# Two graph layers in float32 on one core: head map and messages by seven half-size products, edges turned by DMA, a new order of the first phases

## The chip, the cores and the metric

The kernel runs on one core of a Trainium2 chip. The metric is the device time of one execution in microseconds (us). Five engines work side by side, each through its own queue in order: TensorE (PE, with its weight loads as PEld), VectorE (DVE), ScalarE (ACT), GpSimd (POOL), and SyncE (SP), which only issues DMAs here.

## The reference, cut to what matters

There are 64 graphs of 256 nodes with 512 features, and two attention layers after each other. `adj` is a symmetric boolean matrix per graph, with a true diagonal.

```python
def layer0(embs, score_mask, ...):            # 8 heads of 64
    keep = (~sm[..., 0:1]).astype(embs.dtype)
    m = embs @ map_w.T + map_b
    n = sem / norm                            # m by heads, each row to length 1
    cos_adj = ((n @ n.T) * ~sm > 0.1)
    q, k = m @ q_w.T + q_b, m @ k_w.T + k_b   # by heads
    scores = jnp.where(sm, NEG, q @ k.T / sqrt(64))
    p_attn = softmax(scores) * keep
    adj = cos_adj * p_attn
    sem_h = embs @ gcn_map_w.T + gcn_map_b
    return relu(((adj @ sem_h) @ gcn_W.T) / (adj.sum(-1) + 1))

def layer1(x, adjacency_mask, ...):           # 4 heads of 64
    sim = where(adjacency_mask, q @ k.T / 8, neg)
    return (softmax(sim) @ v) @ Wo + bo

h = relu(layernorm(x));  x = x + layer0(h, adj, ...)
h = relu(layernorm(x));  x = x + layer1(h, adj, ...)
```

Layer 0 attends where there is no edge, layer 1 where there is one.

## The kernel before, in words

Everything is float32. The order of the work is written out by hand: the Python order of the calls is the order in each engine's queue. A software pipeline runs over the graphs. `period(i)` works on up to four of them at once: graph `i` (`g`, the attention of its layer 0 and the projections of its layer 1), graph `i-1` (`b`, the attention of its layer 1 and its output), graph `i+1` (`nx`, map, messages, queries and keys of its layer 0) and graph `i+2` (`n2`, its mask, its layer norm, its transposes). There are 65 periods, of which number 1 to 62 have all of `g`, `b` and `nx`. A prologue, `first(0)` to `first(1)`, fills the pipeline.

The names that matter, in the order of one period, with the lines of the profile:

- `masks` (L286) turns the edges of `n2` by four bf16 transposes on PE into the PSUM tile `p_a`; ACT makes two bf16 masks of it, `mask1` (edges) and `mask0` (1 - edges).
- `turned` (L195, L196): transposes `p_t` of the normalized input, then ACT's relu writes `hT`.
- `spread` (L330, L334): `p_b`, then DVE writes `nT`. `products` (L351): a pair of 64-row products `sc` or `co` per 128 features, two heads side by side, each into a PSUM tile of its own. `exps` (L358, L359): ACT's exponential out of PSUM into `e`, then DVE multiplies by the mask. `halves` (L370): POOL adds the two halves of `e` into `d`. `far` (L365): DVE applies the threshold of the cosine to `e`. `far_off` (L385): POOL adds that to `d`.
- `mapped` (L205, L299, L301): 16 products of 256 columns into `p_m`, DVE adds the bias into `mT`, ACT squares.
- `left_factors` (L219 to L222): POOL makes the four sums `ss` of quarters of `mT` that `seven_products` needs.
- `messages` (L310, L311): per 128 nodes 4 products of 512 columns into `p_s`, then DVE adds the bias into `sem`.
- `queries`, `keys`: `seven_products` (L235, L244, L248, L266), a generator. A 512x512 matrix times `mT` is done as seven products of half-size blocks, each 4 products of 128x128 by 128 columns. Its steps: two products into the PSUM tile `24`, which ACT drains with a bias (`u2`, `u4`); one into tile `z`, which DVE adds to `u2`, then two into tile `53`, drained by ACT (`u5`); one into `z` again, which DVE drains into `uu`; the last into `z`. Each new product into `z` waits until DVE has read the one before.
- `values1`, `sums1`, `values`, `sums` (L377, L402, L443): the weighted sums `av`, and the softmax sums `zb` and `sm`, on PE. `norms` (L317) is `p_n`. `sums_back` (L411): four transposes `rt`. `heads_back` (L424), `result` (L457).
- `p_v`, `p_q`, `p_k` (L552, L205): the projections of layer 1. They end the period.

All PSUM tiles come from one pool, `ring`: eight banks, handed out in turn in the order of the calls. A tile therefore waits until whatever was allocated eight tiles earlier has been read.

Of the kernel before, what the change touches and what calls it, by code (L numbers as in the profile page):

```python
# [28 lines left out]
class Weights:  # L29


    def __init__(self, nc, const, a):
# [4 lines left out]
        self.wm, self.bm = self.load_w("map_wT", "wm"), self.load_b("map_b", "bm")  # L37
# [22 lines left out]
        self.wc = const.tile([P, D // P, D], F32, name="wc")  # L60
# [8 lines left out]
    def load_seven(self, key, name):  # L69


        ap = self.a[key]
        half = ap.shape[0] // 2
        t = self.const.tile([128, 7, half // 128, half], F32, name=name)
        for n, (i, j) in enumerate(((0, 0), (1, 0), (1, 1), (0, 1))):
            block = ap[i * half:(i + 1) * half, j * half:(j + 1) * half]
            self.nc.gpsimd.dma_start(out=t[:, n], in_=block.rearrange("(c p) f -> p c f", p=128))
        return t
# [31 lines left out]
    def fold(self, gws, gbb, bank):  # L110

        nc, P = self.nc, 128
        NKC = self.wc.shape[1]
        nc.vector.tensor_copy(gbb, self.gb[:, :, None].to_broadcast([P, NKC, P]))
        p = bank("p_bc", [P, NKC * P])
        for k in range(NKC):
            nc.tensor.matmul(p[:, k * P:(k + 1) * P], gbb[:, k, :], self.gt, start=True, stop=True)
        nc.vector.tensor_copy(self.bc, p)
        for c in range(NKC):
            p = bank(f"p_wc{c}", [P, NKC * P])  # L120
            for k in range(NKC):
                nc.tensor.matmul(p[:, k * P:(k + 1) * P], gws[k // 2][:, k % 2, c * P:(c + 1) * P], self.gt,
                                 start=True, stop=True)
            nc.vector.tensor_copy(self.wc[:, c, :], p)
# [3 lines left out]
def fast_path(ctx, tc, a, w, chk, out):  # L128
# [61 lines left out]
    def turned(g, tag):  # L190
        hT = sb2.tile([P, NKC, S], F32, tag="hT", name=f"hT{tag}")
# [23 lines left out]
    def left_factors(src, name):  # L215

        a = [src[:, HC * k:HC * (k + 1), t * P:(t + 1) * P] for t in range(2) for k in range(2)]
        ss = sb1.tile([P, 4, HC, P], F32, tag="ss", name=f"ss{name}")
# [6 lines left out]
    def seven_products(left, wt, bias, dst, name):  # L225
# [4 lines left out]
        def product(p, region, block, src):  # L230


            for f in range(HC):
                for c in range(HC):
# [3 lines left out]

        def biased(region, features, what):

            t = sb2.tile([P, HC, P], F32, tag=f"u{what}", name=f"u{what}{name}")
# [5 lines left out]
        def out(tokens, features, x, y):  # L247
            nc.vector.tensor_add(dst[:, HC * features:HC * (features + 1), tokens * P:(tokens + 1) * P], x, y)  # L248

        p24 = bank(f"{name}_24", [P, 2, HC, P])  # L250
# [5 lines left out]
        pz = bank(f"{name}_z", [P, HC, P])  # L256
        product("z", pz, 0, a11)
        out(0, 0, pz, p2)
        p53 = bank(f"{name}_53", [P, 2, HC, P])
# [5 lines left out]
        u4 = sb2.tile([P, HC, P], F32, tag="uu", name=f"uu{name}")  # L265
# [5 lines left out]
        out(1, 0, pz, p4)  # L271


    def edges(g):

        g.adb = sb1.tile([P, NT, S], BF16, tag="adb", name=f"adb{g.i}")
        nc.gpsimd.tensor_copy(g.adb, g.ad)
        g.keep = small.tile([P, NT], F32, tag="keep", name=f"keep{g.i}")
        nc.gpsimd.tensor_scalar(g.keep, g.ad[:, :, 0], -1.0, 1.0, op0=ALU.mult, op1=ALU.add)

    def masks(g):

        pa = bank(f"p_a{g.i}", [P, NT, S], BF16)
        for j in range(NT):
            for t in range(NT):
                nc.tensor.transpose(pa[:, j, t * P:(t + 1) * P], g.adb[:, t, j * P:(j + 1) * P], w.ident_b)  # L286
        g.mask0 = sb2.tile([P, NT * S], BF16, tag="mask0", name=f"mask0_{g.i}")
        g.mask1 = sb2.tile([P, NT * S], BF16, tag="mask1", name=f"mask1_{g.i}", bufs=3)
        paf = pa.rearrange("p j q -> p (j q)")
        nc.scalar.copy(g.mask1, paf)  # L290
        nc.scalar.activation(g.mask0, paf, AF.Copy, scale=-1.0, bias=1.0)

    def mapped(g):
        g.mT = sb1.tile([P, NKC, S], F32, tag="mT", name=f"mT{g.i}")
        g.sq = []
        for n in range(NKC // 2):
            p = features_first(w.wm, g.hT, (2 * n, 2 * n + 1), f"p_m{g.i}_{n}")
            for m in (2 * n, 2 * n + 1):
                nc.vector.tensor_scalar_add(g.mT[:, m, :], p[:, m - 2 * n, :], w.bm[:, m:m + 1])  # L299
            sq = sb2.tile([P, 2, S], F32, tag="sq", name=f"sq{g.i}_{n}")  # L300
            nc.scalar.activation(sq, g.mT[:, 2 * n:2 * n + 2, :], AF.Square)  # L301
            g.sq.append(sq)
        g.left = left_factors(g.mT, f"q{g.i}")

    def messages(g, t):
        if t == 0:
            g.sem = sb2.tile([P, NT, D], F32, tag="sem", name=f"sem{g.i}")
        p = bank(f"p_s{g.i}_{t}", [P, D])
        for c in range(NKC):
            nc.tensor.matmul(p, g.hT[:, c, t * P:(t + 1) * P], w.wc[:, c, :], start=(c == 0), stop=(c == NKC - 1))  # L310
        nc.vector.tensor_add(g.sem[:, t, :], p, w.bc)  # L311

    def norms(g):

        p = bank(f"p_n{g.i}", [P, S])
        for c in range(NKC):
            nc.tensor.matmul(p[32 * c:32 * (c + 1), :], w.blk32, g.sq[c // 2][:, c % 2, :], start=True, stop=True)  # L317
# [18 lines left out]
    def queries(g):  # L336
        g.qT = sb1.tile([P, NKC, S], F32, tag="qT", name=f"qT{g.i}")
        return seven_products(g.left, w.wq, w.bq, g.qT, f"p_q{g.i}")

    def keys(g):  # L340
        g.kT = sb1.tile([P, NKC, S], F32, tag="kT", name=f"kT{g.i}")
        return seven_products(g.left, w.wk, w.bk, g.kT, f"p_k{g.i}")
# [11 lines left out]
    def exps(ps, mask, name):  # L354
# [4 lines left out]
        nc.vector.tensor_mul(e, e, mask[:, None, :].to_broadcast([P, 2, NT * S]))  # L359
        return e  # L360

# [31 lines left out]
    def sums(g):  # L393
        sm = bank(f"sm{g.i}")
        for n in range(2):
            for k in range(4):
# [4 lines left out]
                for m, part in enumerate(parts):  # L401
                    nc.tensor.matmul(sm[32 * k:32 * (k + 1), n, :], w.ones[:, :32], part,  # L402
                                     start=(m == 0), stop=(m == len(parts) - 1))
        nc.scalar.activation(g.sms, sm, AF.Copy, accum_out=chk[:, g.i, 0:1])

    def sums_back(g):

        rt = bank(f"rt{g.i}", [P, NT, 2, P])
        for t in range(NT):
            for n in range(2):  # L410
                nc.tensor.transpose(rt[:, t, n, :], g.sms[:, n, t * P:(t + 1) * P], w.ident)  # L411
        r = small.tile([P, NT * H0], F32, tag="r", name=f"r{g.i}")
        nc.vector.reciprocal(r, rt.rearrange("p t n (k r) -> p (t n k) r", r=32)[:, :, 0])
        rc = small.tile([P, NT * H0], F32, tag="rc", name=f"rc{g.i}")
        nc.scalar.activation(rc, r, AF.Copy, accum_out=chk[:, g.i, 1:2])
        g.rk = small.tile([P, NT, H0], F32, tag="rk", name=f"rk{g.i}")
        for t in range(NT):
            nc.vector.tensor_scalar_mul(g.rk[:, t, :], r[:, t * H0:(t + 1) * H0], g.keep[:, t:t + 1])

    def heads_back(g):  # L420
        for t in range(NT):
# [3 lines left out]
            o = sb2.tile([P, H0, DH], F32, tag="o", name=f"o{g.i}_{t}")  # L425
# [22 lines left out]
    def divided(b):  # L448
        rz = b.rz = sb1.tile([P, NIC, S], F32, tag="rz", name=f"rz{b.i}")
        nc.vector.reciprocal(rz, b.z)  # L450
        b.oT = sb1.tile([P, NIC, S], F32, tag="oT", name=f"oT{b.i}")
        nc.vector.tensor_mul(b.oT, b.avs1, rz)  # L452

    def result(b, t):
        p = bank(f"p_o{b.i}_{t}", [P, D])
        for c in range(NIC):
            nc.tensor.matmul(p, b.oT[:, c, t * P:(t + 1) * P], w.wo1[:, c, :], start=(c == 0), stop=(c == NIC - 1))  # L457
        nc.vector.tensor_add(b.xs[:, t, :], p, b.xs[:, t, :])

    def period(i):  # L460
        g = graphs.get(i) if i < B else None
        b, nx, n2 = graphs.get(i - 1), graphs.get(i + 1), graphs.get(i + 2)

        if g:
            spread(g)
            for c in range(NKC):
                g.e[c] = exps(products(g.kT, g.qT, c, f"sc0_{i}_{c}"), g.mask0, f"0_{i}_{c}")
                g.d[c] = halves(g.e[c], f"0_{i}_{c}")
        if nx:
            mapped(nx)  # L470

        co, sc = {}, {}
        for c in range(NKC):
            if g:
                co[c] = products(g.nT, g.nT, c, f"co{i}_{c}")
            if b and c == 1:
                sc = [products(b.k1T, b.q1T, k, f"sc1_{b.i}_{k}") for k in range(NIC)]
            if g and c < 2:
                far_off(g, c, co[c])
        if b:  # L480
            b.e1 = [exps(sc[k], b.mask1, f"1_{b.i}_{k}") for k in range(NIC)]
# [5 lines left out]
        if nx:  # L487
            messages(nx, 0)
            q = queries(nx)
            for _ in range(3):  # L490
                next(q)
            messages(nx, 1)
            next(q, None)
# [8 lines left out]
        if g:  # L502
            g.avs = sb1.tile([P, NKC, S], F32, tag="wide", name=f"avs{i}")
            g.sms = sb1.tile([P, 2, S], F32, tag="sms", name=f"sms{i}")
# [7 lines left out]
        if b:  # L512
            nc.scalar.activation(b.z, b.rz, AF.Copy, accum_out=chk[:, b.i, 3:4])
# [16 lines left out]
        if nx:  # L530
            nc.scalar.activation(nx.rn, nx.rn, AF.Sqrt)
        if b:
# [9 lines left out]
        if nx:  # L542
            next(k, None)
# [15 lines left out]
        if n2:  # L559
            masks(n2)  # L560
            n2.hT = turned(n2, f"0_{n2.i}")

    with tc.manual_schedule():
        graphs = {0: load(0)}
# [5 lines left out]
        def first(n):  # L570
# [4 lines left out]
            masks(graphs[n])  # L575
            graphs[n].hT = turned(graphs[n], f"0_{n}")

        first(0)
        g = graphs[0]
        mapped(g)  # L580
        w.fold(gws, sb2.tile([P, NKC, P], F32, tag="o", name="gbb"), bank)
        for t in (w.wq, w.wk):
            w.finish_seven(t)
# [4 lines left out]
        messages(g, 0)  # L588
        messages(g, 1)
        q, k = queries(g), keys(g)  # L590
        for step in (q, k) * 4:
            next(step, None)
# [7 lines left out]
def general_path(ctx, tc, a, w, out):  # L600
# [13 lines left out]
    nc.sync.dma_start(out=wq, in_=a["q_wT"].rearrange("(c p) f -> p c f", p=P))  # L614
    wk = one.tile([P, NKC, D], F32, tag="gwk", name="gwk")
# [90 lines left out]

    with tc.For_i(0, B) as b:
# [15 lines left out]
        for m in range(NKC):  # L723
            p = features_first(w.wm, hT, m, f"gp_m{m}")
# [3 lines left out]
        for t in range(NT):  # L728
            p = tokens_first(w.wc, hT, t, f"gp_s{t}")
# [155 lines left out]
```

## Time and profile before

| what | value |
|---|---|
| median of 3 runs | 4013.19 us (4012.94 to 4013.34) |
| the profiled execution, its own time | 4012.99 us |
| its span, first to last instruction | 4011.2 us |
| mean granted TensorE clock | 0.997 |
| PE busy, matmuls | 3960.5 us, 26705 records |
| DVE, POOL, ACT busy | 2403.3, 1976.9, 1464.8 us |
| one period, from one `p_a` to the next | 61.48 us (2026.75 to 2088.23) |

How to read it: busy time of PE is the union of its matmul records, whose ends are modelled, so the difference of two neighbouring starts is the better measure of what a group takes on PE. A float32 matmul leaves two records, so a row "x16" of 128-column products is 8 matmuls.

### The profile page before, as it was taken

Reading aid. Unit: us, or ns where it says so; the run is one execution under the profiler, and the core shown is the slowest. Engines: PE = TensorE matmul, PEld = TensorE weight load, DVE = VectorE, ACT = ScalarE, POOL = GpSimd, SP = SyncE. Lnnn points to the kernel's source line nnn. Section 1 sums busy time; section 2 is a strip of 40 time slices with the busy share of each in tenths; the row PEclk is TensorE's granted clock in tenths of the full one; section 3 lists DMA queues with packets and bytes.
Section 4 is the critical chain, followed back from the end, with each engine's and each line's share of the span. In section 5 each row is a group of like instructions: output and inputs, shape, how many; then the busy total and the mean of one; then the engine's idle time right before and its main releaser. Section 6 shows DMA issues by size and latency. Waiting matters only on the chain.

```text
span 4011.2 us, 64377 instructions
## 1 busy us (share of the span) xinstructions
PE 3960.5 (99%) x26705; PEld 3114.0 (78%) x26705; DVE 2403.3 (60%) x3805; ACT 1464.8 (37%) x3266; POOL 1976.9 (49%) x1548
## 2 busy tenths in 40 slices
PE   7999999999999999999999999999999999999997
PEld 5877778777778777777787777877777877777775
DVE  4665565566566655665666556556656665566564
ACT  2433333333333333333343343333333333333332
POOL 3455455454454553554545545545445455354452
PEclk9999999999999999999999999999999999999998
DMA  2000000000000000000000000000000000000000
GB/s 90 12 23 12 23 12 23 23 12 23 23 12 23 17 18 23 12 23 23 12 23 23 12 23 12 23 23 12 23 23 12 23 17 18 23 12 23 23 6 17
DMA packets 56647, 82.06 MB, mean 20 GB/s; under 512 B 21984, under 2 KB 21984, under 8 KB 56352
## 3 DMA queue, kind: packets, MB, share of 16 engines
q1 hardware_dynamic: 52224, 71.32, 5.6%
q0 software_dynamic: 1856, 6.55, 0.5%
q8 instruction: 211, 3.46, 0.4%
q14 instruction: 84, 0.69, 0.1%
q10 hardware_dynamic: 2272, 0.04, 0.0%
HBM read 44.34 MB, written 33.55 MB: 19 GB/s over the span
## 4 chain that ended last, share of the span: by engine, by line
PE 96%; DVE 0%; ACT 0%; issue 0%; POOL 0%; DVEq 0%; ACTq 0%
PE p_m L205 11%; PE p_s L310 11%; PE av L377 8%; PE sc L351 8%; PE p_k L235 6%; PE co L351 6%; PE p_v L552 6%; PE p_q L235 6%; PE p_k L205 6%; PE p_q L205 6%; PE p_o L457 5%; PE p_k_z L235 4%; PE p_q_z L235 4%; PE p_t L195 3%; PE p_b L330 2%; PE sm L402 2%
## 5 line engine op out<-in xcount | busy, mean ns | idle before, releaser
L370 POOL TENSOR_TENSOR d<-e 128x512 f32<-128x512 f32 x382 | 659.4, 1751 | 1132.0 <-DVE e L359 1132.0
L359 DVE TENSOR_TENSOR e<-e,mask 128x1024 f32<-128x1024 f32 x384 | 618.4, 1665 | 164.6 <-ACT e L358 164.6
L385 POOL TENSOR_TENSOR d<-d,e 128x512 f32<-128x512 f32 x504 | 695.9, 1391 | 19.7
L428 POOL TENSOR_TENSOR xs<-xs,o 128x512 f32<-128x512 f32 x128 | 159.9, 1271 | 640.7 <-DVE o L426 640.7
L310 PE MATMUL p_s<-wc,hT 128*128 128x512 f32 x1024 | 467.0, 599 | 0.0
L205 PE MATMUL p_m<-hT,wm 128*128 128x256 f32 x2048 | 461.8, 384 | 0.7 <-ACT hT L196 0.7
L205 PEld LDWEIGHTS p_m<-hT,wm 128*128 128x128 f32 x2048 | 385.7, 191 | 72.3 <-ACT e L358 20.5
L334 DVE TENSOR_TENSOR nT<-mT,p_b 128x512 f32<-128x512 f32 x128 | 82.3, 684 | 588.1 <-PE p_b L330 588.1
L358 ACT ACTIVATE e<-sc 128x512 f32<-128x512 f32 x768 | 389.7, 617 | 68.2 <-PE sc L351 67.5
L310 PEld LDWEIGHTS p_s<-wc,hT 128*128 128x128 f32 x1024 | 184.5, 190 | 205.4 <-issue 184.7
L365 DVE SCALAR_TENSOR_TENSOR e<-co,e 128x512 f32<-128x512 f32 x512 | 317.2, 680 | 1.9 <-PE co L351 0.5
L541 POOL TENSOR_TENSOR xs<-xs,bo_b 128x512 f32<-128x512 f32 x128 | 171.2, 1356 | 174.9 <-DVE xn L186 172.1
L450 DVE RECIPROCAL rz<-z 128x512 f32<-128x512 f32 x64 | 214.6, 3353 | 71.0 <-ACT z L446 71.0
L351 PE MATMUL co<-nT 64*128 64x256 f32 x2048 | 251.5, 385 | 3.3 <-DVE e L365 3.3
L457 PE MATMUL p_o<-wo,oT 128*128 128x512 f32 x512 | 232.6, 597 | 5.0 <-DVE oT L452 5.0
L377 PE MATMUL av<-e,sem 128*64 128x256 f32 x2048 | 231.9, 379 | 0.0
L552 PE MATMUL p_v<-wv,hT 128*128 128x256 f32 x1024 | 231.7, 379 | 0.2 <-ACT hT L196 0.2
L351 PE MATMUL sc<-qT,kT 64*128 64x256 f32 x2048 | 231.7, 376 | 0.0
L205 PE MATMUL p_q<-hT,wq 128*128 128x256 f32 x1024 | 231.5, 379 | 0.0
L205 PE MATMUL p_k<-hT,wk 128*128 128x256 f32 x1024 | 231.5, 379 | 0.0
L351 PEld LDWEIGHTS co<-nT 64*128 64x128 f32 x2048 | 195.1, 188 | 44.5 <-issue 20.6
L351 PEld LDWEIGHTS sc<-qT,kT 64*128 64x128 f32 x2048 | 198.3, 187 | 22.8
(147 smaller groups left out, 6615.2 us busy)
## 6 DMA issues: line engine op xcount, KB each, us to landing
xs<-in_x_dram SPq DMA_DIRECT2D x64, 512.0 KB, 3.9
out_dram<-xs SPq DMA_DIRECT2D x64, 512.0 KB, 2.8
ad<-in_adj_dram SPq DMA_DIRECT2D x64, 64.0 KB, 3.6
wm<-in_L_gnn_map_w_dram POOLq DMA_DIRECT2D x1, 1024.0 KB, 9.3
gw<-in_L_gnn_gcn_map_w_dram POOLq DMA_DIRECT2D x2, 512.0 KB, 10.2
wq<-in_L_gnn_q_w_dram POOLq DMA_DIRECT2D x4, 256.0 KB, 12.0
wk<-in_L_gnn_k_w_dram POOLq DMA_DIRECT2D x4, 256.0 KB, 8.8
wv<-in_L_gnn_Wv_dram POOLq DMA_DIRECT2D x1, 512.0 KB, 8.5
```

Of the source, the lines that this page charges most:

```text
L205: nc.tensor.matmul(p[:, n, :], wt[:, c, m * P:(m + 1) * P], src[:, c, :], start=(c == 0), stop=(c == nk - 1))
L235: nc.tensor.matmul(region[:, f, :], wt[:, block, c, f * P:(f + 1) * P], src[:, c, :], start=p not in opened, stop=True, skip_group_check=True)
L310: nc.tensor.matmul(p, g.hT[:, c, t * P:(t + 1) * P], w.wc[:, c, :], start=(c == 0), stop=(c == NKC - 1))
L351: nc.tensor.matmul(ps[s][:, j, :], rows[h, c, j * P:(j + 1) * P], cols[h, c, :], start=True, stop=True)
L358: nc.scalar.activation(e[:, s, :], p.rearrange("p j q -> p (j q)"), AF.Exp, scale=SCALE)
L359: nc.vector.tensor_mul(e, e, mask[:, None, :].to_broadcast([P, 2, NT * S]))
L365: nc.vector.scalar_tensor_tensor(e[:, s, :], p.rearrange("p j q -> p (j q)"), THRESHOLD, e[:, s, :], op0=ALU.is_gt, op1=ALU.mult)
L370: nc.gpsimd.tensor_add(d, e[:, :, :S], e[:, :, S:])
L377: nc.tensor.matmul(av[s * DH:(s + 1) * DH, n, :], vs[:, j, (h0 + s) * DH:(h0 + s + 1) * DH], q[:, s, j * S:(j + 1) * S], start=(j == 0), s ...
L385: nc.gpsimd.tensor_add(g.d[c], g.d[c], g.e[c][:, :, j * S:(j + 1) * S])
L457: nc.tensor.matmul(p, b.oT[:, c, t * P:(t + 1) * P], w.wo1[:, c, :], start=(c == 0), stop=(c == NIC - 1))
L552: nc.tensor.matmul(p[:, t, :], hT[:, c, t * P:(t + 1) * P], w.wv1[:, c, :], start=(c == 0), stop=(c == NKC - 1))
```

## The change

- `wm` and the folded message weights `wc` are stored as seven half-size blocks like `wq` and `wk`; `mapped` and `messages` go through `seven_products`. For messages, which have the nodes first, a block product is 2 matmuls of 256 columns, and the biases are added by DVE. POOL makes the sums of quarters for `hT` too (tile `sh`; those for `mT` are now in `sm`, a tile which has nothing to do with the PSUM tile `sm` of the head sums).
- The edges of `n2`: POOL writes `adb` = 1 - edges, and SP's queue turns it by two DMA transposes into one mask. Layer 0 multiplies by it; layer 1 uses mask < 0.5 in a `scalar_tensor_tensor`. `masks` goes.
- The head sums are collected in one row of 256 per 32 partitions in place of two; `sums_back` has two transposes in place of four.
- A one-element exponential right behind the square roots; the reciprocals of layer 1 are made in place.
- Order of a period: the first step of the map ahead of `spread`, the other steps between the mask multiplications; the first step of the messages ahead of `co`; the first step of the queries ahead of `co` 2 and 3; the other steps of queries and messages in turn.
- `hT` has one buffer in place of two. The prologue folds and combines the weights in another order.

```diff
     def seven_products(left, wt, bias, dst, name, tokens_first=False):
...
         def product(p, region, block, src):
-            for f in range(HC):
-                for c in range(HC):
+            for c in range(HC):
+                if tokens_first:
+                    nc.tensor.matmul(region, src[:, c, :], wt[:, block, c, :],
+                                     start=p not in opened, stop=True, skip_group_check=True)
+                    opened.add(p)
+                    continue
+                for f in range(HC):
                     nc.tensor.matmul(region[:, f, :], wt[:, block, c, f * P:(f + 1) * P], src[:, c, :],
                                      start=p not in opened, stop=True, skip_group_check=True)
...
         def biased(region, features, what):
+            t = sb2.tile(shape, F32, tag=f"u{what}", name=f"u{what}{name}")
+            if tokens_first:
+                nc.vector.tensor_add(t, region, bias[:, features * HC * P:(features + 1) * HC * P])
+                return t
...
     def edges(g):
-        g.adb = sb1.tile([P, NT, S], BF16, tag="adb", name=f"adb{g.i}")
-        nc.gpsimd.tensor_copy(g.adb, g.ad)
+        adb = sb1.tile([P, NT, S], BF16, tag="adb", name=f"adb{g.i}")
+        nc.gpsimd.tensor_scalar(adb, g.ad, -1.0, 1.0, op0=ALU.mult, op1=ALU.add)
...
+        g.mask = sb2.tile([P, NT, S], BF16, tag="mask", name=f"mask{g.i}", bufs=3)
+        for t in range(NT):
+            nc.sync.dma_start_transpose(out=g.mask[:, :, t * P:(t + 1) * P], in_=adb[:, t, :])
...
     def mapped(g):
         g.mT = sb1.tile([P, NKC, S], F32, tag="mT", name=f"mT{g.i}")
...
+        return seven_products(g.left_h, w.wm, w.bm, g.mT, f"p_m{g.i}")
+
+    def squares(g):
...
+        g.left_m = left_factors(g.mT, "sm", g.i)
...
-    def messages(g, t):
...
+    def messages(g):
+        g.sem = sb2.tile([P, NT, D], F32, tag="sem", name=f"sem{g.i}")
+        return seven_products(g.left_h, w.wc, w.bc, g.sem, f"p_s{g.i}", tokens_first=True)
...
+    def masked(e, mask, edges):
+        m = mask.rearrange("p j q -> p (j q)")[:, None, :].to_broadcast([P, 2, NT * S])
+        if edges:
+            nc.vector.scalar_tensor_tensor(e, m, 0.5, e, op0=ALU.is_lt, op1=ALU.mult)
+        else:
+            nc.vector.tensor_mul(e, e, m)
...
     def period(i):
...
+        def off_edges(cs):
+            for c in cs if g else ():
+                masked(g.e[c], g.mask, edges=False)
+                g.d[c] = halves(g.e[c], f"0_{i}_{c}")
+        if nx:
+            m, s = mapped(nx), messages(nx)
+            next(m)
         if g:
             spread(g)
             for c in range(NKC):
-                g.e[c] = exps(products(g.kT, g.qT, c, f"sc0_{i}_{c}"), g.mask0, f"0_{i}_{c}")
-                g.d[c] = halves(g.e[c], f"0_{i}_{c}")
+                g.e[c] = exps(products(g.kT, g.qT, c, f"sc0_{i}_{c}"), f"0_{i}_{c}")
+        off_edges((0, 1))
         if nx:
-            mapped(nx)
+            next(m)
+        off_edges((2,))
+        if nx:
+            next(m)
+        off_edges((3,))
+        if nx:
+            next(s)
+            next(m)
+            squares(nx)
 
         co, sc = {}, {}
         for c in range(NKC):
             if g:
                 co[c] = products(g.nT, g.nT, c, f"co{i}_{c}")
             if b and c == 1:
                 sc = [products(b.k1T, b.q1T, k, f"sc1_{b.i}_{k}") for k in range(NIC)]
+            if nx and c == 1:
+                q = queries(nx)
+                next(q)
             if g and c < 2:
                 far_off(g, c, co[c])
         if b:
-            b.e1 = [exps(sc[k], b.mask1, f"1_{b.i}_{k}") for k in range(NIC)]
+            b.e1 = [exps(sc[k], f"1_{b.i}_{k}") for k in range(NIC)]
+            for k in range(NIC):
+                masked(b.e1[k], b.mask, edges=True)
             if not b.last:
                 b.d1 = [halves(b.e1[k], f"1_{b.i}_{k}") for k in range(NIC)]
         if g:
             far_off(g, 2, co[2])
             far_off(g, 3, co[3])
         if nx:
-            messages(nx, 0)
-            q = queries(nx)
-            for _ in range(3):
-                next(q)
-            messages(nx, 1)
-            next(q, None)
+            for step in (q, s, q, s, q, s):
+                next(step)
...
         if nx:
             nc.scalar.activation(nx.rn, nx.rn, AF.Sqrt)
+
+        nc.scalar.activation(spare[:, 1:], spare[:, :1], AF.Exp)
...
         if n2:
-            masks(n2)
-            n2.hT = turned(n2, f"0_{n2.i}")
+            normal_input(n2)
+
+    def normal_input(g):
+        g.hT = turned(g, f"0_{g.i}")
+        g.left_h = left_factors(g.hT, "sh", g.i)
```

## The prediction

> **What bounds the kernel now.** I read the busy shares and the chain of waits first.
>
> ```profile
> PE 3960.5 (99%) x26705; PEld 3114.0 (78%) x26705; DVE 2403.3 (60%) x3805; ACT 1464.8 (37%) x3266; POOL 1976.9 (49%) x1548
> ...
> PE 96%; DVE 0%; ACT 0%; issue 0%; POOL 0%; DVEq 0%; ACTq 0%
> ```
>
> PE is never without work, so PE time removed is time gained, as long as no wait takes its place. Shares over the span don't tell that; the windows of one period, cut at the start of `av` of layer 1, do (columns: length, then busy us of PE, PEld, DVE, ACT, POOL):
>
> ```profile
> 2026.75:2058.27 31.52, 31.52 (x206) 24.74 (x204) 19.97 (x25) 12.96 (x26) 24.14 (x18) 1.00 0.01 1
> 2058.27:2088.23 29.96, 29.96 (x213) 23.66 (x213) 17.38 (x34) 9.87 (x25) 6.80 (x7) 1.00 0.12 39
> ```
>
> All that is reordered lies in the first half, where POOL is busy 24.14 of 31.52 us and DVE 19.97. The timeline of PE in it:
>
> ```profile
> 2026.75 0.39 PE L286 MATMUL p_a<-ident_b,adb 128*128 128x128 bf16 x4
> 2026.98 1.04 PE L195 MATMUL p_t<-ident,xn 128*128 128x128 f32 x8
> 2027.95 1.14 PE L330 MATMUL p_b<-rn,sel 64*128 64x256 f32 x8
> ...
> 2032.47 7.17 PE L205 MATMUL p_m<-hT,wm 128*128 128x256 f32 x32
> 2039.57 2.00 PE L351 MATMUL co<-nT 64*128 64x256 f32 x16
> ...
> 2044.95 3.70 PE L310 MATMUL p_s<-wc,hT 128*128 128x512 f32 x8
> 2048.49 1.95 PE L235 MATMUL p_q<-mT,wq 128*128 128x128 f32 x16
> 2050.28 1.06 PE L235 MATMUL p_q_z<-mT,wq 128*128 128x128 f32 x8
> ```
>
> From start to start: `p_a` 0.23, `p_m` 7.10, `p_s` 3.54 (its second half 3.43), two block products 1.79, one 0.89. Two more views carry the argument: when ACT drains a tile `24`, and how long mask products (L359) and POOL's sums (L370) take, shortest, median and longest.
>
> ```profile
> 2050.48 0.63 ACT L244 ACTIVATE u2p_q<-p_q,bq 128x128 f32<-128x128 f32 x2 [5.89 <-PE p_q L235]
> ```
>
> ```profile
> L359 DVE TENSOR_TENSOR e<-e,mask x6: 1221/1486/2297, 2032.4 to 2044.8; 128x1024 f32<-128x1024 f32 x6
> ```
>
> ```profile
> L370 POOL TENSOR_TENSOR d<-e x6: 1268/1731/2247, 2033.7 to 2052.8; 128x512 f32<-128x512 f32 x6
> ```
>
> ACT starts 0.20 after both products of the tile (2050.28), not after the first. Mask products and POOL's sums each come short or a whole instruction longer: they take turns.
>
> **What the Trainium skill says.** "SBUF — State Buffer", section "Who interferes with whom": a VectorE instruction with two SBUF inputs and a GpSimd instruction that reads SBUF exclude each other for the whole instruction. The trace agrees (1221 alone, 2297 behind POOL). "TensorE: Matmul & The Clock Gate", "Step-by-step: what each phase is for": only weight loads are pulled ahead, matmuls stay in program order; the orderly chain shows nothing else. "ScalarE: Activation LUTs", "What ACT_TABLE_LOAD costs": about 1283 ns each; here 1283 (L358). "DMA: Bandwidth & Descriptors", "Latency and other measured facts": 261 GB/s for DMA transposes; no run here shows one.
>
> **The change part by part: PE work removed, per graph.** `p_m`: 28 products of 128 columns, 7 x 0.893 = 6.25 in place of 7.10: -0.85. `p_s`: 14 products of 256 columns at 0.4325 (`p_v`, L552: 8 in 3.46) = 6.06 in place of 6.97: -0.91. `p_a`: -0.23. Two of the four `rt` (0.44): -0.22. The head sums keep 8 matmuls. Sum -2.2 per graph, -139 in 63 graphs.
>
> **What is added beside PE.** DVE gets about 2.2 us per period (13 operations of 256 columns at 0.42 for 4 at 0.47 and 2 at 0.68), POOL four sums for `hT` (0.73 each), ACT six small drains, less two masks (0.6 each). The table load moves from ahead of the exponentials to behind the roots: ACT idles 2.23 us there (2013.04 to 2015.26), 1.28 + 0.2 fit. That gains nothing: PE never waited for these exponentials. DMA transposes: estimated from the skill's figure, 128 KB take 0.5 us per graph. On SP they wait for POOL's `adb` (about 2 us after `av` of layer 1 starts) with the output (17 us later) and the next loads queued behind. Their cover is time: the mask and those loads are needed a period later, and `adb` is rewritten a period later. Below, they cost nothing; above, only if the two take a period, some 30 us each. I take nothing. In-place reciprocals remove no instruction; with one `hT`, its writer waits for `p_k` (0.20), and `k1T` holds ACT longer: nothing. Second-half chains keep their order and margins (`oT` is done 1.5 us before `rt`).
>
> **The first half walked through.** Latencies from this trace: PE to ACT 0.20, PE to DVE 0.27 (128-column group), ACT to DVE 0.04, ACT or DVE to PE 0.06. ACT exponentials follow every 0.48 to 0.49. Time 0 is the end of `p_k`.
>
> *Wait 1.* `p_t` ends at 0.88. ACT first copies `k1T` (from 0.20), then starts `hT` at 0.69 and ends its first half at 1.31, so PE starts the map's first step at 1.37: 0.49 lost. Before, `p_b` and `sc` covered that.
>
> `p_b` follows at 3.16, `nT` is done 5.6, `sc` runs 4.13 to 7.68, exponentials 5.22 to 9.25. DVE's masks: 6.34 to 7.57; to 8.71; then the map's `z` into `mT` 8.84 to 9.27; third mask behind POOL's first `d` until 10.92; `uu` and `mT` to 12.40; fourth mask behind POOL until 14.37; two drains and two adds until 15.72. PE in between: `z` 8.57, `53` 10.36, `z` 11.25, messages' `24` 12.98, `z` 13.87, `co` 0 and 1 15.70: each operand is ready in time, with about 1 us to spare. `sc` of layer 1 waits 0.08 for a bank. It ends 17.51, the queries' `24` ends at E = 19.30.
>
> *Wait 2.* ACT's queue now holds `u2` and `u4` of the queries ahead of layer 1's exponentials. They wait for both products: E + 0.20. Four drains take 1.03 (2050.48 to 2051.51), so the first exponential ends at E + 1.83. In the ring, the second tile of `co` 3 reuses the bank of that `sc`, and PE is there at E + 0.89. It resumes at E + 1.89; one of four matmuls being already done, `co` 3 ends at E + 2.78 in place of E + 1.82: 0.96 lost.
>
> *Wait 3.* DVE must mask both `e` of layer 1 and do four `far` (0.60 each) before it reads the queries' `z`. First pair of exponentials: E + 2.31. POOL is then in its unbroken row of `far_off` sums (from 18.7, every 1.2 to 1.35); DVE finds one running until about E + 3.28 (w = 0.93; 0 to 1.27 is possible). Mask 1.09, a POOL sum between them 1.13, mask 1.09, four `far`, one add (0.43): the bank is free at E + 8.51 + w. PE (0.89 + 1.79 + 0.87 + 1.73 after `co` 3) is there at E + 8.05. Lost: 0.46 + w = 1.39, bounds 0.46 and 1.73. Queued behind: all remaining steps of queries and messages, and `av` after them.
>
> A PE that resumes after a wait also runs its first products slower:
>
> ```profile
> 3981.11 2.00 PE L351 MATMUL sc<-q1T,k1T 64*128 64x256 f32 x16 [0.68 <-ACT k1T L558]
> ```
>
> (1.89 without a wait): 0.1 each, 0.3 together, bounds 0 and 0.3. Waits in all: 0.49 + 0.08 + 0.96 + 1.39 + 0.3 = 3.22, bounds 1.99 and 3.56. Without waits the first half adds up to 29.34 by the starts (31.52 less 1.99, and less 0.19 by which `p_t` and `p_m` ran slower where they stood). With them 29.34 + 3.22 = 32.56; the second half 29.96 - 0.22 = 29.74; **period 62.30 in place of 61.48: +0.82**, for 62 periods +51.
>
> **Ends.** Prologue: `p_t` no longer waits for POOL (20.73), but the map's fifth product waits for `sh` behind 22 DMA issues on POOL, the messages wait for combined `wc` and for DVE, which combines `wq` and `wk` (8 x 0.72) ahead of the messages' drains: the first queries' product moves from 47.04 to some 53 (estimate, 0 to +8): +6. Period 0 has no `b`: -1. The last two periods: -2 (no table load ahead of the last exponentials, fewer `rt`). Sum +54: 4012.99 + 54 = 4067. The profiled execution is 0.2 below the median, so this holds for the median too.
>
> **Rivals.** *No third wait*: if POOL doesn't step between the two masks of layer 1 (or DVE meets a free port), DVE reads `z` by E + 7.4, before PE comes at E + 8.05, and 1.39 + 0.1 disappear. For it: POOL's position is worked out over 20 us. Against: L359 shows turns wherever both have work. Period 60.81: 4067 - 62 x 1.49 = 3975, faster. It decides at a third of a POOL sum (0.46 us). *No wait at all*, PE stays bound: 4013 - 139 + 3 = 3877; for it the 99%; against, the drains ahead of the exponentials, which is an order and no estimate. *More waits*: the steps in between have 1 us to spare, and mask products with a comparison could be slower than L359; 0.8 more per period: 4117. *The transposes don't keep up*: at over 30 us each every period would last as long as its two, far above 4117; the skill's figure speaks against it.
>
> **How the numbers follow.** Three waits as walked 0.70 (its own range 3990 to 4100: w and restart at their bounds give -76 and +21, second-half margins and prologue the rest); no third wait 0.12; none 0.06; more waits 0.10; transposes 0.02. About 0.2% (8 us) is what a measurement can tell from no change. Faster: 0.12 + 0.06 + 0.03 of the first case; within: 0.06; slower: the rest. The range 3975 to 4115 leaves out the case without waits, half of no third wait, half of more waits and the transposes: 0.19.
>
> **What would show it.** Right: `p_m` and `p_s` groups of 0.89 per block product; idle PE ahead of the map's first step (0.5), `co` 3 (released by ACT's `e`, 1.0) and the queries' second `z` (released by DVE, about 1.4) in all 62 periods; period near 62.3. Wrong: PE 99% busy with a period near 59.3, or a POOL sum absent between the two masks.

## The result and the profile after

The changed kernel takes 4064.01 us (median of 4 runs, 4062.55 to 4066.96) against 4013.07 for the kernel before on the same chip (4 runs, 4011.56 to 4013.34): ratio 1.0129, interval 1.0111 to 1.0146. It is slower by about 51 us although PE has less to compute. The page's busy line of PE and its chain:

```profile
PE 3931.1 (97%) x28625; PEld 3259.8 (80%) x28625; DVE 2523.3 (62%) x4269; ACT 1501.1 (37%) x3587; POOL 2100.0 (52%) x1807
...
PE 81%; DVE 9%; ACT 5%; issue 2%; POOL 0%; DVEq 0%; ACTq 0%
```

PE busy fell by 29 us only, not by 139, and the chain, 96% PE before, now runs through DVE and ACT for 14%. The windows of one period, cut at the same place as before (length, then busy us of PE, PEld, DVE, ACT, POOL):

```profile
1995.65:2028.16 32.51, 31.23 (x238) 27.16 (x236) 21.74 (x32) 12.25 (x29) 25.82 (x22) 1.00 0.01 1
2028.16:2057.90 29.74, 29.74 (x211) 23.47 (x211) 17.43 (x34) 11.15 (x27) 6.98 (x7) 1.00 0.14 43
```

The second half lost its 0.22 (29.96 to 29.74); the first grew from 31.52 to 32.51, and PE stands idle in it for 1.28 us. Where, shows the timeline of PE (start, length, then idle time just before it and who ended it; a length with no idle time may hold a short stall inside):

```profile
2013.54 2.05 PE L258 MATMUL p_q<-mT,wq 128*128 128x128 f32 x16
2015.52 2.49 PE L371 MATMUL co<-nT 64*128 64x256 f32 x16
2017.94 1.16 PE L258 MATMUL p_q_z<-mT,wq 128*128 128x128 f32 x8
...
2024.45 1.16 PE L258 MATMUL p_q_z<-sm,wq 128*128 128x128 f32 x8 [0.97 <-DVE qT L280]
...
2057.90 1.04 PE L212 MATMUL p_t<-ident,xn 128*128 128x128 f32 x8
2059.25 2.05 PE L258 MATMUL p_m<-hT,wm 128*128 128x128 f32 x16 [0.31 <-ACT hT L213]
```

These are the three waits: `p_t` to the map's first step 1.35 from start to start; `co` 2 and 3 2.42 (2015.52 to 2017.94) where `co` 0 and 1 take 1.83; and the queries' second `z`, released by DVE. That they come in every period, the view of waits says (us in total, times, longest; PE's own waits, then its weight loads'). Of the loads, `co` shows wait 2. A load that starts a step whose semaphore is already set shows about 0.3 us too (`p_m_z`: 20.5 us in 62 times), although PE itself loses only 0.1 there (`p_m_z` 0.99 in place of 0.89):

```profile
PE p_q_z L258 <- DVE qT L280: 59.8, 62, 1.2
PE p_m L258 <- ACT hT L213: 19.5, 63, 0.3
```

```profile
PEld p_q_z L258 <- DVE qT L280: 84.7, 62, 1.6
PEld p_m L258 <- ACT hT L213: 34.7, 64, 0.6
PEld p_q_z L258 <- ACT e L378: 20.6, 62, 0.3
PEld p_m_z L258 <- ACT e L378: 20.5, 62, 0.3
PEld co L371 <- ACT u4p_q L272: 12.7, 62, 0.2
```

The next views answer to the drains and the mask products shown of before: ACT's timeline, then the instructions on `e` in the first half (shortest, median, longest ns; first and last start).

```profile
2015.69 0.63 ACT L272 ACTIVATE u2p_q<-p_q,bq 128x128 f32<-128x128 f32 x2 [2.98 <-PE p_q L258]
2016.21 0.63 ACT L272 ACTIVATE u4p_q<-p_q,bq 128x128 f32<-128x128 f32 x2
2016.71 2.08 ACT L378 ACTIVATE e<-sc 128x512 f32<-128x512 f32 x4
```

```profile
L412 POOL TENSOR_TENSOR d<-d,e x8: 1258/1272/2129, 2014.5 to 2027.9; 128x512 f32<-128x512 f32 x8
L385 DVE SCALAR_TENSOR_TENSOR e<-mask,e x2: 1620/1952/2284, 2017.8 to 2019.4; 128x1024 f32<-128x1024 bf16 x2
```

The four drains of the queries' first step stand ahead of layer 1's exponentials; both masks of layer 1 are longer than the 1220 of a free one, and one of POOL's sums is stretched to 2129: the two engines took turns.

### The profile page after: what moved, and what is told of

The parts are those of the page before. It is cut to its first block, busy times and chain, and to the rows that moved or that the text cites. A ratio compares the mean times of both kernels' runs of the same rounds, so it can differ in the third digit from the quotient of the medians.

```text
span 4060.0 us, 70097 instructions
## 1 busy us (share of the span) xinstructions
PE 3931.1 (97%) x28625; PEld 3259.8 (80%) x28625; DVE 2523.3 (62%) x4269; ACT 1501.1 (37%) x3587; POOL 2100.0 (52%) x1807
## 4 chain that ended last, share of the span: by engine, by line
PE 81%; DVE 9%; ACT 5%; issue 2%; POOL 0%; DVEq 0%; ACTq 0%
PE av L404 8%; PE sc L371 8%; PE p_m L258 6%; PE p_k L258 6%; PE p_v L596 5%; PE p_k L222 5%; PE p_q L222 5%; PE p_o L482 5%; DVE e L385 5%; PE p_m_z L258 4%; PE p_k_z L258 4%; DVE e L392 3%; PE p_q_z L258 3%; PE p_q L258 3%; PE co L371 3%; PE p_s_z L253 3%
## 5 line engine op out<-in xcount | busy, mean ns | idle before, releaser
L412 POOL TENSOR_TENSOR d<-d,e 128x512 f32<-128x512 f32 x504 | 688.1, 1376 | 19.8
L236 POOL TENSOR_TENSOR sh<-hT 128x256 f32<-128x256 f32 x64 | 46.3, 723 | 797.6 <-ACT hT L213 797.6
L387 DVE TENSOR_TENSOR e<-e,mask 128x1024 f32<-128x1024 f32 x256 | 386.7, 1532 | 48.8 <-ACT e L378 48.8
L385 DVE SCALAR_TENSOR_TENSOR e<-mask,e 128x1024 f32<-128x1024 bf16 x128 | 241.8, 1928 | 256.9 <-ACT e L378 256.9
L371 PE MATMUL co<-nT 64*128 64x256 f32 x2048 | 288.0, 395 | 2.6 <-DVE e L392 2.6
L476 DVE RECIPROCAL z<-z 128x512 f32<-128x512 f32 x64 | 214.6, 3353 | 62.9 <-ACT z L473 62.9
L371 PEld LDWEIGHTS co<-nT 64*128 64x128 f32 x2048 | 205.2, 186 | 49.5 <-ACT u4p_q L272 12.7
L462 ACT COPY avs<-av 128x512 f32<-128x512 f32 x64 | 37.5, 586 | 543.4 <-PE av L404 543.4
L482 PE MATMUL p_o<-wo,avs 128*128 128x512 f32 x512 | 232.8, 598 | 5.0 <-DVE avs L477 5.0
L222 PEld LDWEIGHTS p_q<-hT,wq 128*128 128x128 f32 x1024 | 194.6, 190 | 26.4
```

Source lines behind the costliest of these rows:

```text
L222: nc.tensor.matmul(p[:, n, :], wt[:, c, m * P:(m + 1) * P], src[:, c, :], start=(c == 0), stop=(c == nk - 1))
L371: nc.tensor.matmul(ps[s][:, j, :], rows[h, c, j * P:(j + 1) * P], cols[h, c, :], start=True, stop=True)
L385: nc.vector.scalar_tensor_tensor(e, m, 0.5, e, op0=ALU.is_lt, op1=ALU.mult)
L387: nc.vector.tensor_mul(e, e, m)
L412: nc.gpsimd.tensor_add(g.d[c], g.d[c], g.e[c][:, :, j * S:(j + 1) * S])
L482: nc.tensor.matmul(p, b.avs1[:, c, t * P:(t + 1) * P], w.wo1[:, c, :], start=(c == 0), stop=(c == NIC - 1))
```

## The experiments

Each ran against the kernel before (4011.5 us in the first four, 4012.4 in the last three, medians of 7 runs).

**1. Layer 1's exponentials first.** They are issued right behind their `sc`, ahead of the queries' first step.

```diff
             if b and c == 1:
                 sc = [products(b.k1T, b.q1T, k, f"sc1_{b.i}_{k}") for k in range(NIC)]
+                b.e1 = [exps(sc[k], f"1_{b.i}_{k}") for k in range(NIC)]
             if nx and c == 1:
                 q = queries(nx)
                 next(q)
...
-            b.e1 = [exps(sc[k], f"1_{b.i}_{k}") for k in range(NIC)]
```

> The changed kernel, with the exponentials of layer 1 called right behind their products, ahead of the first step of the queries. My theory (ACT's queue holds the queries' drains ahead of these exponentials, which makes co 3 wait 0.60 us and the queries' second z 1.13 us in each of 62 periods, plus about 0.1 for the restart): both waits go, 1.8 us x 62 = 112 us less, near 3952 us. Rival (DVE and GpSimd simply have too much to do in the first half, whatever the order): the waits move to a later step and the time stays within 20 us of 4064.

Measured: 3955.65 us, ratio 0.9859 (0.9842 to 0.9875). PE's timeline in this kernel:

```profile
2023.66 2.05 PE L258 MATMUL p_q<-mT,wq 128*128 128x128 f32 x16
2025.64 2.00 PE L371 MATMUL co<-nT 64*128 64x256 f32 x16
2027.57 1.16 PE L258 MATMUL p_q_z<-mT,wq 128*128 128x128 f32 x8
...
2032.94 1.05 PE L258 MATMUL p_q_z<-sm,wq 128*128 128x128 f32 x8
```

`co` 2 and 3 take 1.93 in place of 2.42, and the second `z` comes without a wait. The period is 60.53 in place of 62.25: 0.49 of wait 2, 1.13 of wait 3 and 0.10 by which the step behind wait 3 had started slower make the 1.72. One line's place in ACT's queue costs 108 us.

**2. The map's first step behind `p_b`** (`next(m)` after `spread(g)`), so that the copy of `hT` has `p_b` for cover.

```diff
             m, s = mapped(nx), messages(nx)
-            next(m)
         if g:
             spread(g)
+        if nx:
+            next(m)
+        if g:
             for c in range(NKC):
```

> The changed kernel, with the first step of the map behind spread in place of ahead of it, so that p_b (0.97 us on PE) covers ScalarE's writing of hT. My theory: the wait of 0.47 us and a slow restart of 0.1 go, 0.5 to 0.6 us x 62 = 31 to 37 us less, near 4030. Rival (the gain is eaten by the exponentials, which follow ACT's drains of that step): within 8 us of 4064.

Measured: 4053.43 us, ratio 1.0102 (1.0085 to 1.0118): only 10.6 less, a third of what was expected; theory and rival both missed. PE's timeline:

```profile
2053.86 1.04 PE L212 MATMUL p_t<-ident,xn 128*128 128x128 f32 x8
2054.83 1.13 PE L350 MATMUL p_b<-rn,sel 64*128 64x256 f32 x8
2055.89 2.05 PE L258 MATMUL p_m<-hT,wm 128*128 128x128 f32 x16
2057.88 3.72 PE L371 MATMUL sc<-qT,kT 64*128 64x256 f32 x32
2061.53 0.71 PE L258 MATMUL p_m_z<-hT,wm 128*128 128x128 f32 x4
```

The wait is gone: `p_t` to the next step is 0.97 where it was 1.35. But `p_b` now takes 1.06 from start to start (0.97 in the changed kernel), and `sc` 3.65 (3.55). So 0.38 was won and 0.19 given back in two steps of 0.1: the period is 62.07, 0.18 shorter. The 0.47 that the wait seemed to cost was counted from `p_t`'s 0.88 with no wait behind it; a step that begins with a wait, here one already fulfilled, costs about 0.1 by itself.

**3. POOL's sums of the first two `far_off` behind layer 1's masks.** DVE's masks then find no sum running.

```diff
         far(co, g.e[c])
-        if not g.last:
+        if c > 1:
+            far_sums(g, c)
+
+    def far_sums(g, c):
+        if not g.last:
...
                 b.d1 = [halves(b.e1[k], f"1_{b.i}_{k}") for k in range(NIC)]
+        if g:
+            for c in range(2):
+                far_sums(g, c)
```

> The changed kernel, with GpSimd's four sums of far_off for the first two feature groups moved behind the masks and halves of layer 1; nothing else moves. My theory (the third wait comes from GpSimd sums that stand in the way of VectorE's two masks, 0.5 + 1.1 us): the third wait of 1.13 and its restart go, 1.2 us x 62 = 76 us less, near 3988. Rival (VectorE's own queue of two masks and four thresholds is too long by itself): at most 0.3 us x 62 = 19 us less. A second possibility: GpSimd is then late for the head sums, since it ends only 0.2 us ahead of them, which would give some back.

Measured: 3989.14 us, ratio 0.9943 (0.9927 to 0.996), period 61.01. Layer 1's masks, and the queries' second `z` in PE's timeline:

```profile
L385 DVE SCALAR_TENSOR_TENSOR e<-mask,e x2: 1220/1223/1226, 2042.6 to 2043.8; 128x1024 f32<-128x1024 bf16 x2
```

```profile
2048.09 1.05 PE L258 MATMUL p_q_z<-sm,wq 128*128 128x128 f32 x8
```

With the masks at 1.22 us each wait 3 is gone (1.13 and the 0.10 behind it, of 62.25), though the exponentials come as late as in the changed kernel. In experiment 1 the sums still stretched the masks (1708 and 2289 ns), and the wait was gone all the same. Wait 3 thus needs both: late exponentials and POOL's sums around the masks. The comparison itself is no slower than the plain mask product of before (1221).

**4. No one-element exponential.** Its line goes, and the table load stands ahead of the exponentials again.

```diff
-        nc.scalar.activation(spare[:, 1:], spare[:, :1], AF.Exp)
```

> The changed kernel without the one-element exponential, so that the table load of 1.28 us stands ahead of the first exponentials again. If the first half has only about 1 us to spare, as I walked it through: everything behind the exponentials comes 1.28 us later, and PE waits for VectorE's reading of the map's z, 0.5 to 1.4 us more per period, 30 to 87 us more, 4095 to 4150. Rival (the load is hidden wherever it stands, as it was in the kernel before): within 8 us of 4064.

Measured: 4050.03 us, ratio 1.0093 (1.0076 to 1.011): 14 less; theory and rival both missed. Four views of it: ACT's timeline, POOL's, layer 1's masks, and PE's timeline at the second `z`.

```profile
2054.93 1.28 ACT L378 ACT_TABLE_LOAD   x1 [0.82 <-PE sc L371]
```

```profile
2069.30 7.03 POOL L412 TENSOR_TENSOR d<-d,e 128x512 f32<-128x512 f32 x4
```

```profile
L385 DVE SCALAR_TENSOR_TENSOR e<-mask,e x2: 1241/1763/2285, 2071.8 to 2072.9; 128x1024 f32<-128x1024 bf16 x2
```

```profile
2077.98 1.16 PE L258 MATMUL p_q_z<-sm,wq 128*128 128x128 f32 x8 [0.59 <-DVE qT L280]
```

The load delays the exponentials by 1.28, but DVE had been idle for 0.8 us in this stretch of the changed kernel, waiting for PE's `z` (0.15 and 0.68 ahead of two drains), and no longer is; its third and fourth mask also take 0.2 less together (3.47 for 3.69). So the messages' drains come only 0.05 later, and PE loses 0.04. POOL's row of sums (L412) starts 0.9 later in the period. DVE therefore meets a sum about to end (first mask 1241) in place of one in its first half (1620), and wait 3 is 0.38 shorter. That is all of the 0.33 per period, 20 us in 62 periods; the prologue and the last two periods take some 7 of them back. It is a matter of phase and no merit of the table load.

**5. Only the edges and the head sums, in the kernel before.**

```diff
-        pa = bank(f"p_a{g.i}", [P, NT, S], BF16)
...
+        for t in range(NT):
+            nc.sync.dma_start_transpose(out=g.mask[:, :, t * P:(t + 1) * P], in_=adb[:, t, :])
```

> The kernel before with one part of the change alone: edges turned by DMA into one mask (no p_a, no second mask, the comparison in layer 1) and head sums in two rows per 32 with two rt transposes. Products and order stay those of before. Theory (this part only takes PE work away, 0.23 + 0.22 us per period, and its transposes are hidden): period 61.48 - 0.45 = 61.03, 29 us less, and some 10 less in the prologue, where p_t no longer waits for POOL: 3974, within 10. Rival (the comparison or the transposes cost time themselves): 4000 or more, with a new wait in front of av or of the mask products.

Measured: 3976.33 us, ratio 0.9909 (0.9893 to 0.9926), period 61.03: the two terms, 0.23 and 0.22, come out whole, and the prologue gives the rest. This part is pure gain; the transposes are hidden.

**6. The seven half-size products in the order of before.**

```diff
-        off_edges((0, 1))
-        if nx:
-            next(m)
...
+        off_edges((0, 1, 2, 3))
+        if nx:
+            for _ in range(4):
+                next(m)
...
+            q = queries(nx)
+            for step in (s, q, q, q, s, s, s, q):
+                next(step)
```

> The changed kernel with the order of before: the map's five steps stand together behind the four mask products, the queries begin only behind the last far_off, so layer 1's exponentials are ahead of the queries' drains in ACT's queue. The seven half-size products stay. Theory (the order makes the waits, not the products): waits 1, 2 and 3 are gone; in their place DVE, with four masks ahead of the map's drains, may hold a bank for up to some 2 us. Period 59.4 to 61.5, likeliest 60.3: 3944, between 3890 and 4020. Rival (half-size products bring their drains and sums, and these cost the time in any order): period 62.2 or more, 4060 or more.

Measured: 4189.05 us, ratio 1.0437 (1.042 to 1.0455), periods of 63.3 to 65.1. My theory missed by 245 us, of which some 60 are a halved clock in 42 periods (last section). The rival had the right side, but not the reason: experiments 1 and 7 show orders in which the half-size products don't cost the time. PE's timeline, and DVE's:

```profile
2064.58 1.95 PE L258 MATMUL p_m<-sh,wm 128*128 128x128 f32 x16
2068.11 1.16 PE L258 MATMUL p_m_z<-sh,wm 128*128 128x128 f32 x8 [1.58 <-DVE mT L280]
2069.85 1.16 PE L258 MATMUL p_m_z<-sh,wm 128*128 128x128 f32 x8 [0.59 <-DVE uup_m L298]
```

```profile
2060.48 7.24 DVE L387 TENSOR_TENSOR e<-e,mask 128x1024 f32<-128x1024 f32 x4 [0.76 <-ACT e L378]
2067.64 0.41 DVE L280 TENSOR_TENSOR mT<-p_m_z,u2p_m 128x256 f32<-128x256 f32 x1
```

Four masks, taking turns with POOL, hold DVE for 7.24 us, and the map's first drain stands behind them; the map's next `z` waits for that drain. The one large product of before needed no drain in between. So the half-size products need steps between the masks, as the change has them; waits 2 and 3 of the changed kernel come from the queries' early step, wait 1 from the map's, and not from all of its order.

**7. Moves 1 and 2 together**, and in the prologue `wq` and `wk` combined only behind the map's second step.

```diff
         next(m)
+        for t in (w.wq, w.wk):
+            w.finish_seven(t)
...
-        for t in (w.wq, w.wk):
-            w.finish_seven(t)
```

> The changed kernel with three moves: layer 1's exponentials ahead of the queries' first step (3955.7 alone), the map's first step behind p_b (0.18 us per period less by itself), and in the prologue wq and wk combined only behind the map's second step. Theory: the gains add, since they lie at different places: 3955.7 - 11 - 4 = 3941, within 6, period 60.35. Rival (a gain of 0.18 is taken back where waits 2 and 3 no longer cover it): 3952 or more.

Measured: 3939.62 us, ratio 0.9818 (0.9801 to 0.9834), period 60.34: faster than both kernels. The page:

```profile
PE 3890.6 (99%) x28625; PEld 3242.2 (82%) x28625; DVE 2548.1 (65%) x4269; ACT 1505.3 (38%) x3587; POOL 2103.6 (53%) x1807
...
PE 96%; DVE 1%; POOL 0%; ACT 0%; issue 0%; ACTq 0%; DVEq 0%
```

Of the 16 us below experiment 1, 0.18 x 63 = 11 are the period's; the first product of the queries starts at 49.2 in place of 53.0, which is 4. The chain is PE's again, at the 96% of before.

## Why the prediction was right, and where its terms were off

The median forecast was 4067, measured 4064; period 62.30 against 62.25, its halves 32.56 and 29.74 against 32.51 and 29.74. The three waits are there, at the places named. The losses of the first half come to 32.51 - 29.34 = 3.17 in place of 3.22, but the terms within them were further off and cancelled. That the median came within 3 us is luck in that respect:

- **Wait 1**: 0.49 predicted, 1.35 - 0.88 = 0.47 measured, in the sense of the prediction. Experiment 2 took back less than half of it (0.18).
- **Bank of layer 1's `sc`**: 0.08 predicted, nothing measured. `sc` takes 1.82 where it took 1.73, but its own products follow each other without a gap; the 0.09 lies behind the last of them, at the start of the queries' step, and is a restart.
- **Wait 2**: 0.96 predicted, 2.42 - 1.82 = 0.60 measured, and the releaser was wrong. I let the second tile of `co` 3 take the bank of the tile eight places earlier, a tile of `sc`. PE goes on at 2016.88, when `u4` has ended (2016.83) and the first exponential has not (2017.32); the view of waits names `u4`, the last reader of the queries' `p_q` for `24`. So `co` 3 got that bank, and the eight banks aren't handed out strictly in turn, as the section on the kernel before has it. That the bank goes whose release stands first in the program would fit; it was not tried. The exponentials hold PE one step later: its queue waits from 2017.39 to 2017.85 for the second of them (2017.81) ahead of the queries' first `z`, in all 62 periods, which is just when `co` is through. I estimate from these times that with another bank for `co` 3 about 0.5 of the 0.60 would have stayed.
- **Wait 3**: 1.39 predicted, 1.13 measured (2023.32, when PE could have gone on, to 2024.45). The mechanism is the one described (late exponentials, a mask, a POOL sum, a mask, four `far`, a drain); its w was 0.54, not 0.93, as POOL's row ran 0.4 us earlier. POOL's earlier row made it smaller, and the shorter wait 2, by which PE comes earlier, larger. Experiments 1 and 3 take away one of its two conditions each, and it goes.
- **Restarts**: 0.3 predicted, 3.17 - 0.47 - 0.60 - 1.13 = 0.97 measured. This is the term that was most wrong. I charged 0.1 to each of the three long waits, and took 0.19 of the same kind out of `p_t` and `p_m` of before without asking where it would come back. The trace shows it at steps whose semaphore had already been set too: `p_m` and `p_q` for `24` take 1.98 (1.79 elsewhere), a `z` that begins so 0.99 (0.89). Waits 2 and 3 and the bank, 0.70 too large together, and this term, 0.67 too small, cancelled.
- **Removed work**: -2.2 per graph was right (block products of 0.89, `p_s` 0.87 per block), and experiment 5 shows its smaller part exactly. Yet the version in which all three waits are gone has a period of 60.34, not 59.3: about 1.1 of the 2.2 goes to such starts (in that version `p_b` +0.09, `p_m` +0.19, `sc` +0.11, two `z` of the map +0.19, `sc` of layer 1 +0.09, `p_q` +0.19, `co` +0.11, the queries' first `z` +0.11, against the same steps without one), as the products are cut into steps that begin with a wait. By that the rival of 3877 was out of reach even without the waits.
- **What was costed at nothing**: each transpose lands 2.3 us after its issue (page, below; I had estimated 0.5 for the two), with a period to spare, and experiment 5 shows no loss. Moving the table load gains nothing, as said; experiment 4, without the move, was even 14 us faster, by the phase of POOL.
- **"About 1 us to spare"** in the steps between: held without a new wait there, and a delay of 1.28 in experiment 4 cost 0.04. My expectation for that run took the margin for rigid; a VectorE that itself waits for PE's next product gives time back.
- **Ends**: 4064.0 - 4013.1 = 51, less 62 x 0.77 = 48, leaves +3, as in the sum (+3). The queries' first product starts at 52.43 (some 53 predicted, 47.04 before).

The line of the DMA part of the page, median us from issue to landing:

```profile
mask<-adb SPq DMA_TRANSPOSE x128, 2.3
```

## What to carry to other kernels

Work taken from the bounding engine is won only if every smaller piece finds its drain in time: look at what stands ahead of the drain in the queues of the other engines, not at their busy shares. A step brought forward also brings its drains forward in an in-order queue, here ahead of exponentials on which a longer chain hung; issuing the exponentials first was worth 108 us. And count a start cost for each step that begins with a wait (0.1 us here) before cutting one product into seven.

## What the runs showed of the hardware that was not expected

A stretch of short waits halves TensorE's clock, without one long pause. In experiment 6, two pairs of neighbouring windows at the same stall of two periods (the third column from the end is the granted clock):

```profile
1937.43:1940.84 3.41, 1.43 (x10) 1.25 (x11) 2.06 (x4) 0.49 (x2) 3.35 (x2) 1.00 0.00 0
1940.84:1944.26 3.42, 3.42 (x18) 2.85 (x19) 0.88 (x3) 1.02 (x2) 0.83 (x2) 0.50 0.00 0
2067.14:2070.55 3.41, 1.85 (x14) 1.67 (x15) 1.76 (x4) 0.05 (x1) 2.93 (x2) 1.00 0.00 0
2070.55:2073.96 3.41, 3.41 (x33) 3.00 (x33) 2.54 (x5) 1.22 (x3) 1.93 (x3) 1.00 0.02 5
```

After 1.43 us of work in 3.41 the clock stood at half for the next 3.41 us; after 1.85 it stayed full. The Trainium skill ("TensorE: Matmul & The Clock Gate", "Part 1: The HAM clock gate") says that the clock drops after an idle window of about 3.4 us, and that these windows run freely. Here the longest pause at the stall is about 1.6 us, so a window needn't be empty.

The stall is nearly the same in all of the 62 periods after the first, but 20 of them stay at full clock (63.3 us and less) and the other 42 take 64.6 or more. Free-running windows explain which. The clock records of the trace change only on a grid of 3.413 us. These 62 periods cut on that grid show it: in the windows ahead of all 42 halvings PE was busy for 1.39 to 1.76 us, and in every other window at full clock for 1.77 or more. So it depends on whether one window takes in most of the stall or two windows share it. The limit is that of this stretch: in the prologue of experiment 1 a window with 1.52 us of work is not followed by half clock, so the busy time of the records can't be the whole measure.

The 0.1 us at the start of a step whose wait is already fulfilled shows in the timelines of both kernels (`p_t` 0.97 and 0.88 before, `z` 0.99 and 0.89 after) and of the experiments. That a weight load isn't pulled ahead across a wait would be the reason, but this was argued and not tried.
